# Earlier loads of transposed rows in linear attention, and attention weights copied to PSUM for VectorE's weighing

## The chip, the cores and the metric

The kernel runs on one core of one Trainium2 chip. A core has TensorE (PE, matrix multiplications, with its weight loads shown apart as PEld), VectorE (DVE), ScalarE (ACT), GpSimd (POOL) and SyncE (SP), each with its own instruction stream, and 16 DMA engines that move data between HBM and the on-chip memories SBUF and PSUM. Streams are in order: an instruction that waits holds up what stands behind it on its engine. The metric is the device time of one execution in microseconds (us).

## The reference

One block of a graph network over 6250 nodes with 256 features and 200000 edges sorted by destination. Cut to what matters:

```python
xn = layernorm(x)
x = x + gnn(xn, edge_index) + mix(xn)
x = x + ffn(layernorm(x))            # 8 experts, top 2

# gnn: three layers; heads 4, 4, 1
xh = (h @ W).reshape(n, heads, d)
alpha = leaky_relu((xh * att_src).sum(-1)[src] + (xh * att_dst).sum(-1)[dst])
e = exp(alpha - segment_max(alpha, dst)[dst])
alpha = e / segment_sum(e, dst)[dst]
out = segment_sum(xh[src] * alpha[:, :, None], dst)   # then + bias, layernorm, residual, relu

# mix: linear attention, 8 heads of 32
q, k, v = split(xn @ Wqkv.T);  q, k = elu(q) + 1, elu(k) + 1
kv = einsum("shd,shm->hmd", k, v)
t = q . kv / (q . sum(k))
x1 = layernorm(t + xn) ;  y = gelu(x1 @ W1.T + b1) @ W2.T + b2
mix = layernorm(y + x1)
```

## The kernel before

**Stages.** After planning the edges and projecting the nodes for the first layer (up to about 190 us), the kernel runs the three graph layers one after the other. The edges are laid out in rows of 128; 32 rows make a supertile, and each layer has 52 supertiles, worked in 16 steps each by `sum_messages`. A step takes two rows of edges.

**One supertile.** POOL gathers the rows of source nodes by indirect DMA, one instruction for each row of 128 edges (`gather`, L536), into tiles `g` of eight rows; 8 such tiles are in turn in layer 0, 9 in layer 1. The next gather into a tile waits until PE has read it. From the gathered scores the generator `maxima` computes the softmax weights of the supertile ahead, in pieces that are advanced in steps 9 to 14: ACT copies the scores out of `g` (L593), PE and VectorE take running maxima (L603 to L655), VectorE forms the exponents `w` (L666), ACT takes the exponential (L678), and VectorE writes each row's turn values into `g` (L684). In layers 0 and 1 (4 heads) `weigh` then multiplies the gathered rows with `w`: of each four rows ACT does two (L700, one instruction for each head), VectorE the other two in one instruction (L693). PE sums the rows by destination with one-hot matrices (`pair`, L730), which VectorE makes by comparing lane numbers (L559); for that comparison a copy of the lane numbers, `lane_ps`, lies in PSUM. VectorE adds the sums to `acc` (L743). Layer 2 has one head, and there ACT weighs all rows.

**Work beside.** Everything else is cut into pieces by `yield`, and `Beside.step` takes pieces from a queue at each step, in layer 0 at 1.25 pieces a step. In layer 0 the queue first holds `linear_attention`, then the updates of blocks of nodes as they are complete; in layer 2 it holds the experts. `Order` keeps on each engine the order of the text.

**Linear attention.** Two passes over 13 groups of node blocks (the first of one block, the others of four). Each group's normalized, transposed rows come from HBM (`xnt`) into the tile `et` by `load_xt`. The first pass forms keys and values (L1050) and sums their product; the second forms queries (L1106) into `qt`, multiplies (L1115), normalizes, transposes the result into `at` (another use of the tile `et`, L1138), runs the two layers W1 (L1145, into `ht`, another use of the tile `qt`) and W2 (L1154, with `at` added by L1157), normalizes again and stores the group to `res`. All these tiles have one buffer. In both passes the load stands at the head of a group; the loads are issued on SP, in the order of the text, so in the second pass it comes behind the store of the group before (L1169):

```python
    for g, (t0, n) in enumerate(groups()):      # second pass, L1090
        w = n * P
        xt = load_xt(g, n)
        x = wk.tile([P, GRP, C + 2 * HEADS], F32, name="ea")[:, :, :C]
        Where(tc, t0, n).load(x, i["x"])
        yield
```

Of the kernel before, what the change touches and what calls it, by code (L numbers as in the profile page):

```python
# [7 lines left out]
F32 = mybir.dt.float32  # L8
# [5 lines left out]
PS = bass.MemoryType.PSUM  # L14

P = 128
# [22 lines left out]
GRP = 4  # L39
# [433 lines left out]
def sum_messages(tc, pools, consts, q, node_rows, adn, h, acc, beside, slot, order):  # L473
# [7 lines left out]
    nc = tc.nc  # L481
    lp, tb, gp, hp, tp, wk, pmp, smp = pools
# [7 lines left out]
    half = GRP // 2 if h > 1 else 0  # L490
# [14 lines left out]
    T, A, M = {}, {}, {}  # L505
# [90 lines left out]
    def maxima(s):  # L596

        m, t = M[s], T[s]
# [3 lines left out]
        at = smp.tile([P, P], F32, name="sm")  # L602
# [62 lines left out]
        w = m["w"] = wk.tile([P, h, SU], F32, name="w")  # L665
# [12 lines left out]
        nc.scalar.activation(w, w, AF.Exp)  # L678
        nc.scalar.activation(fac, fac, AF.Exp)
        yield  # L680

        for k in range(subs):
            i = slice(k * SUB, (k + 1) * SUB)
# [4 lines left out]
    def weigh(s, c, n, engine):  # L688

        t, k, w = rows[s * subs + c // SUB], c % SUB, M[s]["w"]  # L690
        if engine is nc.vector:
            x = t[:, k:k + n, :body].rearrange("p c (h d) -> p c h d", h=h)
            nc.vector.tensor_tensor(  # L693
                x, x, w[:, :, c:c + n].rearrange("p h c -> p c h")[:, :, :, None].to_broadcast(
                    [P, n, h, d1]), op=OP.mult)
            return
        for i in range(n):
            for j in range(h):
                x = t[:, k + i, j * d1:(j + 1) * d1]
                nc.scalar.activation(x, x, AF.Copy, scale=w[:, j, c + i:c + i + 1])  # L700
# [57 lines left out]
    for s in range(-1, NS):  # L758
        n = s + 1
# [202 lines left out]
def groups():  # L962

    return [(0, 1)] + [(t0, GRP) for t0 in range(1, NB, GRP)]
# [60 lines left out]
def linear_attention(tc, pools, consts, i, mean, rstd, xnt, res):  # L1025

    nc = tc.nc
    mp, wk, sm, psum = pools
# [9 lines left out]
    def load_xt(j, n):  # L1038
        xt = wk.tile([P, 2, GRP * P], F32, name="et")
        load(tc, xt[:, :, :n * P], xnt[j, :, :, :n * P])  # L1040
        return xt

    for g, (t0, n) in enumerate(groups()):
        xt = load_xt(g, n)
        yield
        pk = psum.tile([P, 2, P + 1], F32, name="fk")
        for t in range(n):
            pt = psum.tile([P, 512], F32, name="fa")
            for k in range(2):
                nc.tensor.matmul(pt, xt[:, k, t * P:(t + 1) * P], wkv[:, k, :],  # L1050
                                 start=(k == 0), stop=(k == 1))
            yield
            low = elu_low(tc, wk, pt[:, :C])
            val = wk.tile([P, 2, P + 1], F32, name="val1")
            nc.vector.memset(val[:, :, P:], 1.0)
            nc.scalar.copy(val[:, :, :P], pt[:, C:].rearrange("p (j d) -> p j d", j=2))
            yield
            key = wk.tile([P, C], F32, name="key1")
            elu_join(tc, pt[:, :C], low, key)
            if t0 + t == 0:  # L1060
                nc.vector.memset(key[:SHIFT], 0.0)
            yield
            for j in range(2):
                nc.tensor.matmul(pk[:, j, :], key[:, j * P:(j + 1) * P], val[:, j, :],
                                 start=(t == 0 and j == 0), stop=(t == n - 1 and j == 1))
        yield
        nc.vector.tensor_add(kvs, kvs, pk)
# [4 lines left out]
    for j in range(2):  # L1072
        for q in range(4):
            s = slice(q * 32, (q + 1) * 32)
# [14 lines left out]

    for g, (t0, n) in enumerate(groups()):  # L1090
        w = n * P
        xt = load_xt(g, n)
        x = wk.tile([P, GRP, C + 2 * HEADS], F32, name="ea")[:, :, :C]
        Where(tc, t0, n).load(x, i["x"])
        yield
        qt = wk.tile([P, 2, GRP * P], F32, name="qt")
        pts, low = {}, None
        for j in range(3):
            if low is not None:
                elu_join(tc, pts[j - 2][:, :w], low, qt[:, j - 2, :w])  # L1100
            if j:
                low = elu_low(tc, wk, pts[j - 1][:, :w])
            if j < 2:
                pts[j] = psum.tile([P, 512], F32, name=("fa", "fk")[j])
                for k in range(2):
                    nc.tensor.matmul(pts[j][:, :w], wq[:, k, j * P:(j + 1) * P], xt[:, k, :w],  # L1106
                                     start=(k == 0), stop=(k == 1))
            yield
        elu_join(tc, pts[1][:, :w], low, qt[:, 1, :w])
        yield  # L1110
        a = wk.tile([P, GRP, C], F32, name="eo")
        for t in range(n):
            pt = psum.tile([P, 2, P + 4], F32, name=("fa", "fk")[t % 2])
            for j in range(2):
                nc.tensor.matmul(pt[:, j, :], qt[:, j, t * P:(t + 1) * P], kvm[:, j, :],  # L1115
                                 start=True, stop=True)
            yield
            z = sm.tile([P, 2, 4], F32, name="z")
            nc.vector.tensor_scalar(z, pt[:, :, P:], 1e-6, None, op0=OP.add)
            nc.vector.reciprocal(z, z)  # L1120
            nc.vector.tensor_tensor(
                a[:, t, :].rearrange("p (j h d) -> p j h d", j=2, d=32),
                pt[:, :, :P].rearrange("p j (h d) -> p j h d", d=32),
                z[:, :, :, None].to_broadcast([P, 2, 4, 32]), op=OP.mult)
            xn = wk.tile([P, C], F32, name="xn")
            nc.vector.tensor_scalar(xn, x[:, t, :], mean[:, t0 + t, 0:1],
                                    rstd[:, t0 + t:t0 + t + 1], op0=OP.subtract, op1=OP.mult)
            nc.vector.tensor_add(a[:, t, :], a[:, t, :], xn)
        yield
        yield from norm_pieces(tc, sm, consts, a, n)  # L1130
        at = wk.tile([P, 2, GRP * P], F32, name="et")
        for k in range(2):
            pt = psum.tile([P, 512], F32, name=("fa", "fk")[k])
            for t in range(n):
                nc.tensor.transpose(pt[:, t * P:(t + 1) * P], a[:, t, k * P:(k + 1) * P],
                                    consts["ident"])
            yield
            nc.scalar.activation(at[:, k, :w], pt[:, :w], AF.Identity,  # L1138
                                 scale=cols["ln1_g"][:, k:k + 1], bias=cols["ln1_b"][:, k:k + 1])
        yield  # L1140
        ht = wk.tile([P, 2, GRP * P], F32, name="qt")
        for j in range(2):
            pt = psum.tile([P, 512], F32, name=("fa", "fk")[j])
            for k in range(2):
                nc.tensor.matmul(pt[:, :w], w1[:, k, j * P:(j + 1) * P], at[:, k, :w],  # L1145
                                 start=(k == 0), stop=(k == 1))
            yield
            nc.scalar.activation(ht[:, j, :w], pt[:, :w], AF.Gelu, bias=cols["b1"][:, j:j + 1])
        yield
        for t in range(n):  # L1150
            s = slice(t * P, (t + 1) * P)
            pt = psum.tile([P, 512], F32, name=("fa", "fk")[t % 2])
            for k in range(2):
                nc.tensor.matmul(pt[:, :C], ht[:, k, s], w2[:, k, :], start=(k == 0), stop=False)  # L1154
            nc.tensor.matmul(pt[:, :C], ones[0:1, :], b2, start=False, stop=False)
            for k in range(2):
                nc.tensor.matmul(pt[:, k * P:(k + 1) * P], at[:, k, s], consts["ident"],  # L1157
                                 start=False, stop=(k == 1))
            yield
            nc.scalar.copy(a[:, t, :], pt[:, :C])  # L1160
        yield
        yield from norm_pieces(tc, sm, consts, a, n)
        row(tc, a[:, :n], ln2_g, n, OP.mult)
        yield
        row(tc, a[:, :n], ln2_b, n, OP.add)
        yield
        nc.vector.tensor_add(a[:, :n], a[:, :n], x[:, :n])
        yield
        Where(tc, t0, n).store(res, a)  # L1169
# [3 lines left out]
def graph_block(ctx, tc, i, out):  # L1173
    nc = tc.nc
# [3 lines left out]
    consts = make_consts(tc, cp)  # L1178
# [28 lines left out]
    with tc.tile_pool(name="ord", bufs=1) as tmp, \  # L1207
# [6 lines left out]
        n = unordered(tc, tmp, psum, consts, i["dst"])  # L1214
# [19 lines left out]
    for l, h in enumerate(heads):  # L1234
        W = C + 2 * h
        with ExitStack() as lc:
            def pool(name, bufs, **kw):
                return lc.enter_context(tc.tile_pool(name=name, bufs=bufs, **kw))
# [3 lines left out]
            nc.vector.memset(acc, 0.0)  # L1242
            lp, tb, gp = pool("lay", 1), pool("tables", 4), pool("rows", (8, 9, 7)[l])
            hp, tp, wk = pool("hots", 4), pool("hots_t", 3), pool("scores", 2)
            consts["lane_ps"] = pool("lane_ps", 1, space=PS).tile([P, P], F32, name="lane_ps")
            nc.vector.tensor_copy(consts["lane_ps"], consts["lane"])
            pmp, smp = pool("pm", 3, space=PS), pool("smp", 2, space=PS)
            ew, es, eps_ = pool("nodes", 1), pool("nodes_sm", 2), pool("nodes_ps", 1, space=PS)
            mw = pool("moe_w", 3) if l == 2 else None
# [358 lines left out]
```

## Time and profile before

| | |
|---|---|
| median of 3 runs | 7555.33 us (7549.93 to 7557.84) |
| the profiled execution | 7542.13 us, span 7540.3 us |
| busy, share of the span | PE 76%, PEld 52%, DVE 62%, ACT 46%, POOL 66% |
| granted TensorE clock, mean | 0.823 |
| gathers in layers 0, 1, 2 | from 188 to 2470, 2544 to 4737, 4807 to 7358 us |
| HBM read, written | 1024.89 MB, 56.03 MB |

The span is the time from the first to the last instruction of one profiled execution; busy time is the sum of an engine's instruction rows. Rows of the profile's groups give line, engine, operation, tiles (out<-in, buffer numbers left out), shapes and count, then busy us and the mean ns of one, then the engine's idle time just before them and what ended most of it. In timelines each row has start us, duration us, and in brackets the idle time before it and what ended it. "issue" is time in which the engine waited for nothing that the profile shows. Answers for a single line give the shortest, median and longest duration in ns.

### The profile page before, as it was taken

To read this page: it belongs to the slowest core of one execution; us is meant where nothing else is said; L and a number is where in the kernel's file an instruction comes from. 1 tells how busy PE (TensorE), PEld (TensorE's weight loads), DVE (VectorE), ACT (ScalarE), POOL (GpSimd) and SP (SyncE) were. 2 spreads that over 40 slices of the span, in tenths; PEclk is the share of its full clock that TensorE was granted. 3 is DMA by queue.
4 is the path that set the end of the run, shared out by engine and by line. 5 is a ranking of instruction groups with operands and counts; after the bars stand their busy time and mean duration, and the time that the engine had idled before them with its cause. 6 is when DMAs were issued, how large, how long until landed. Compare 5 with 4: busy or idle time off the path is not lost. (4 is left out here: it accounts for less than half of the span.)

```text
span 7540.3 us, 99268 instructions
## 1 busy us (share of the span) xinstructions
PE 5705.6 (76%) x24919; PEld 3900.4 (52%) x24919; DVE 4692.9 (62%) x13293; ACT 3442.0 (46%) x10810; POOL 4995.5 (66%) x5019
## 2 busy tenths in 40 slices
PE   5687878777766366666666666369999999999998
PEld 3455545455444244434444444246666666666666
DVE  5567777788866466656666666455555655555552
ACT  2455555555444244444444444234545544544543
POOL 0777666677777477777777777476665666666660
PEclk8798888877777677777777777679999999999999
DMA  4555444455555454545545555455555555555563
GB/s 149 151 156 151 134 141 132 141 146 162 150 147 133 90 145 138 143 137 146 143 140 146 141 146 135 90 142 163 165 158 157 160 154 155 158 154 161 159 149 90
DMA packets 627785, 1086.34 MB, mean 144 GB/s; under 512 B 200127, under 2 KB 355155, under 8 KB 627198
## 3 DMA queue, kind: packets, MB, share of 16 engines
q0 software_dynamic: 240288, 671.72, 33.9%
q1 hardware_dynamic: 386910, 408.03, 18.1%
q8 instruction: 217, 3.56, 0.2%
q14 instruction: 370, 3.03, 0.1%
HBM read 1024.89 MB, written 56.03 MB: 143 GB/s over the span
## 5 line engine op out<-in xcount | busy, mean ns | idle before, releaser
L536 POOL DMA_INDIRECT g<-node_rows,src_t x4992 | 4979.1, 997 | 2298.4 <-issue 1362.2
L730 PE MATMUL pm<-g,hot 128*128 128x264 f32 (+1 forms) x9984 | 3281.1, 463 | 759.6 <-ACT g L700 396.8
L730 PEld LDWEIGHTS pm<-g,hot 128*128 128x128 f32 x9984 | 2080.4, 224 | 1484.0 <-ACT g L700 491.6
L700 ACT ACTIVATE g<-g,w 128x65 f32<-128x65 f32 (+1 forms) x8320 | 2399.3, 369 | 0.1
L743 DVE TENSOR_TENSOR acc<-acc,pm 128x264 f32 (+1 forms) x2496 | 1048.6, 420 | 222.1 <-PE pm L730 199.9
L593 ACT COPY asc<-g 128x32 f32<-128x32 f32 (+1 forms) x624 | 140.5, 225 | 1609.8 <-DMA g<-node_rows,src_t 1609.6
L559 DVE TENSOR_TENSOR hot<-lane_ps,lane_t 128x1024 f32<-128x1024 f32 x624 | 758.6, 1216 | 0.0
L607 DVE TENSOR_TENSOR_SCAN mx_f<-cut_t,sm 128x128 f32<-128x128 bf16 (+1 forms) x156 | 64.6, 414 | 953.9 <-PE sm L603 953.7
L693 DVE TENSOR_TENSOR g<-g,w 128x520 f32<-128x520 f32 x832 | 575.4, 692 | 3.7 <-issue 1.4
L603 PE MATMUL sm<-ident,asc 128*128 128x128 f32 (+1 forms) x156 | 59.8, 383 | 586.3 <-ACT asc L593 586.2
L586 PEld LDWEIGHTS <-hot_t 128*128 128x128 bf16 x4992 | 310.3, 99 | 281.6 <-DVE hot_t L551 75.4
L1524 ACT ACTIVATE moe_h<-fa,moe_b 128x512 f32<-128x512 f32 (+1 forms) x208 | 137.7, 662 | 614.8 <-PE fa L1519 614.2
L1531 PE MATMUL fa<-moe_w,moe_h 128*128 128x256 f32 x1600 | 394.5, 389 | 17.3 <-ACT moe_h L1524 15.5
L1519 PE MATMUL fa<-et,moe_w 128*128 128x512 f32 (+1 forms) x832 | 394.8, 598 | 6.5 <-DVE eo L1536 4.0
L1519 PE MATMUL fk<-et,moe_w 128*128 128x512 f32 (+1 forms) x832 | 382.3, 582 | 15.4 <-DVE eo L1536 8.0
L1531 PE MATMUL fk<-moe_w,moe_h 128*128 128x256 f32 x1536 | 372.1, 385 | 0.9 <-DVE eo L1536 0.9
L586 PE MATMUL sm<-adc,hot_t 128*128 128x12 bf16 (+1 forms) x4992 | 325.1, 178 | 45.8 <-DVE hot_t L551 40.5
L603 PEld LDWEIGHTS sm<-ident,asc 128*128 128x128 f32 (+1 forms) x156 | 23.0, 147 | 649.4 <-ACT asc L593 647.4
L1531 PEld LDWEIGHTS fa<-moe_w,moe_h 128*128 128x128 f32 x1600 | 293.4, 191 | 66.3 <-ACT moe_h L1524 24.5
L551 DVE TENSOR_SCALAR hot_t<-hot_t,pidx 128x1024 bf16<-128x1024 bf16 x624 | 301.6, 483 | 37.4 <-DMA hot_t<-q_lane_rows 37.1
L1531 PEld LDWEIGHTS fk<-moe_w,moe_h 128*128 128x128 f32 x1536 | 283.0, 190 | 39.4 <-DVE eo L1536 1.7
L1536 DVE SCALAR_TENSOR_TENSOR eo<-fa,share,eo 128x256 f32<-128x256 f32 x200 | 96.1, 481 | 317.8 <-PE fa L1531 317.5
(370 smaller groups left out, 5643.5 us busy)
## 6 DMA issues: line engine op xcount, KB each, us to landing
hot_t<-q_lane_rows SPq DMA_DIRECT2D x624, 256.0 KB
moe_w<-in_L_ffn_W_dram SPq DMA_DIRECT2D x208, 512.0 KB
g<-node_rows,src_t POOLq DMA_INDIRECT x4992
ea<-node_rows SPq DMA_DIRECT2D x24, 528.0 KB
et<-xnt SPq DMA_DIRECT2D x24, 512.0 KB
hid<-eo SPq DMA_DIRECT2D x24, 512.0 KB
eold<-hid SPq DMA_DIRECT2D x24, 512.0 KB
node_rows<-r SPq DMA_DIRECT2D x12, 528.0 KB
```

The costliest lines, as they stand in the source:

```text
L536: nc.gpsimd.indirect_dma_start(out=t[:, c, :], out_offset=None, in_=node_rows, in_offset=bass.IndirectOffsetOnAxis(ap=T[s]["src"][:, i:i + ...
L551: nc.vector.tensor_scalar(lanes[m], lanes[m], consts["pidx"], None, op0=OP.is_equal)
L559: nc.vector.tensor_tensor(t, consts["lane_ps"][:, None, :].to_broadcast([P, SUB, P]), T[s]["lane"][:, k * SUB:(k + 1) * SUB, None].to_broa ...
L586: nc.tensor.matmul(m["ex"][:, c], lanes[s * subs + c // SUB][:, c % SUB, :], adc(s)[:, :, :, c // 2], start=True, stop=True)
L593: nc.scalar.copy(m["asc"][:, :, k * SUB:(k + 1) * SUB].rearrange("p h c -> p c h"), rows[s * subs + k][:, :, body:])
L693: nc.vector.tensor_tensor(x, x, w[:, :, c:c + n].rearrange("p h c -> p c h")[:, :, :, None].to_broadcast([P, n, h, d1]), op=OP.mult)
L700: nc.scalar.activation(x, x, AF.Copy, scale=w[:, j, c + i:c + i + 1])
L730: nc.tensor.matmul(pm, m["hots"][2 * i // SUB][:, k + j, :], t[:, k + j, :], start=(j == 0), stop=(j == 1))
L743: nc.vector.tensor_tensor(at, at, pm, op=OP.add)
L1519: nc.tensor.matmul(pt[:, :w], w1[:, k, j * P:(j + 1) * P], xt[:, k, :w], start=(k == 0), stop=(k == 1))
L1524: nc.scalar.activation(hx[:, j, :w], pt[:, :w], AF.Gelu, bias=self.b1[:, e * 4 + j:e * 4 + j + 1])
L1531: nc.tensor.matmul(pt[:, :C], hx[:, j, t * P:(t + 1) * P], w2[:, j, :], start=(j == 0), stop=(j == 3))
```

## The change

In `linear_attention` the load of a group's transposed rows moves from the head of the group to the end of the group before it, behind the last matmul that reads the tile. The first load, and the one for the second pass's first group, have places of their own; in the first pass one `yield` stands before the loop in place of one in each group. In the second pass `at` and `ht` swap tiles, so that the tile `et` is free for the next rows after the last L1154 of a group. In `maxima`, for layers with more than one head, VectorE copies `w` after the exponential into PSUM, into one of two halves by turns, and VectorE's weighing reads that copy; ACT's weighing reads `w` as before. The PSUM tile of the lane numbers grows by these two halves, within its bank.

```diff
 # maxima
         nc.scalar.activation(w, w, AF.Exp)
         nc.scalar.activation(fac, fac, AF.Exp)
         yield
+        if half:
+            m["w_ps"] = consts["w_ps"][:, s % 2].rearrange("p (h c) -> p h c", h=h)
+            nc.vector.tensor_copy(m["w_ps"], w)
 
 # weigh
         if engine is nc.vector:
+            w = M[s].get("w_ps", w)
             x = t[:, k:k + n, :body].rearrange("p c (h d) -> p c h d", h=h)
 
 # linear_attention, first pass
+    xt = load_xt(0, 1)
+    yield
     for g, (t0, n) in enumerate(groups()):
-        xt = load_xt(g, n)
-        yield
...
                 nc.tensor.matmul(pt, xt[:, k, t * P:(t + 1) * P], wkv[:, k, :],
                                  start=(k == 0), stop=(k == 1))
+            if t == n - 1:
+                xt = load_xt(g + 1, GRP) if g + 1 < len(groups()) else load_xt(0, 1)
             yield
 
 # linear_attention, second pass
         w = n * P
-        xt = load_xt(g, n)
...
-        at = wk.tile([P, 2, GRP * P], F32, name="et")
+        at = wk.tile([P, 2, GRP * P], F32, name="qt")
...
-        ht = wk.tile([P, 2, GRP * P], F32, name="qt")
+        ht = wk.tile([P, 2, GRP * P], F32, name="et")
...
                 nc.tensor.matmul(pt[:, k * P:(k + 1) * P], at[:, k, s], consts["ident"],
                                  start=False, stop=(k == 1))
+            if t == n - 1 and g + 1 < len(groups()):
+                xt = load_xt(g + 1, GRP)
             yield
 
 # graph_block
-            consts["lane_ps"] = pool("lane_ps", 1, space=PS).tile([P, P], F32, name="lane_ps")
+            ps = pool("lane_ps", 1, space=PS).tile([P, 3, P], F32, name="lane_ps")
+            consts["lane_ps"] = ps[:, 0]
             nc.vector.tensor_copy(consts["lane_ps"], consts["lane"])
+            consts["w_ps"] = ps[:, 1:]
```

## The prediction

> **What bounds the kernel now.** I read the page's busy table and costliest groups first, then the busy time by stage, then what the gathers waited for in each stage, then single gathers beside VectorE. The page:
>
> ```profile
> PE 5705.6 (76%) x24919; PEld 3900.4 (52%) x24919; DVE 4692.9 (62%) x13293; ACT 3442.0 (46%) x10810; POOL 4995.5 (66%) x5019
> ...
> L536 POOL DMA_INDIRECT g<-node_rows,src_t x4992 | 4979.1, 997 | 2298.4 <-issue 1362.2
> L693 DVE TENSOR_TENSOR g<-g,w 128x520 f32<-128x520 f32 x832 | 575.4, 692 | 3.7 <-issue 1.4
> ```
>
> No engine is busy throughout, and POOL's 66% hides that it is the bound for half of the span: of its idle time 1362.2 us are "issue", a pause behind each gather in which it waits for nothing. Busy time by stage (columns: window, its us, then PE, PEld, DVE, ACT, POOL; the windows are layer 0 with attention's first pass, attention's second pass, layer 0's rest, layer 1, layer 2):
>
> ```profile
> 260.00:700.00 440.00, 359.87 (x1633) 235.19 (x1631) 295.53 (x866) 245.32 (x918) 335.06 (x345) 0.90 0.55 151
> 700.00:1500.00 800.00, 620.56 (x2731) 411.70 (x2731) 586.41 (x1596) 424.10 (x1394) 540.44 (x547) 0.82 0.49 139
> 1500.00:2480.00 980.00, 682.89 (x2910) 470.24 (x2910) 720.78 (x1992) 470.02 (x1747) 737.98 (x717) 0.73 0.55 146
> 2600.00:4700.00 2100.00, 1351.88 (x5867) 901.10 (x5866) 1353.90 (x3683) 911.79 (x3632) 1613.89 (x1596) 0.74 0.51 142
> 4900.00:7350.00 2450.00, 2277.47 (x10008) 1592.39 (x10009) 1403.25 (x4195) 1183.44 (x2524) 1553.70 (x1584) 0.94 0.56 157
> ```
>
> In layer 1 one gather starts every 2100/1596 = 1.316 us. The gather's own row for 2700 to 4600 us shows what of that is unavoidable:
>
> ```profile
> L536 POOL DMA_INDIRECT g<-node_rows,src_t x1444: 942/946/2479, 2699.3 to 4599.2; - x181
> ...
>   issue: 384.2, 1261
> ```
>
> Median 946 ns, and 0.30 us of pause behind each: 1.25 us at best. The pauses never exceed that pair in layer 1 (summed excess over 304 ns: 1.1 us), while ACT's L593 waits 791 us for gathers to land. So layer 1 is bound by POOL, and so are the first window (excess pause 0.2 us) and the third (14 us). The second isn't: there POOL's pauses exceed 304 ns by 94 us, waiting for row buffers that PE has not yet read. Layer 2 is bound by PE.
>
> Why do gathers take 1012 ns on average in layer 1 where the median is 946? POOL and then VectorE at one place (start, duration):
>
> ```profile
> 3150.05 1.49 POOL L536 DMA_INDIRECT g<-node_rows,src_t  x1 [0.30 <-issue]
> 3151.85 0.94 POOL L536 DMA_INDIRECT g<-node_rows,src_t  x1 [0.30 <-issue]
> ```
>
> ```profile
> 3150.03 0.69 DVE L693 TENSOR_TENSOR g<-g,w 128x520 f32<-128x520 f32 x1
> 3150.64 0.42 DVE L743 TENSOR_TENSOR acc<-acc,pm 128x264 f32 x1
> 3150.98 1.21 DVE L559 TENSOR_TENSOR hot<-lane_ps,lane_t 128x1024 f32<-128x1024 f32 x1
> ```
>
> The gather at 3150.05 is 0.54 us too long: L693 was running 0.13 us after its start and ended at 3150.72, 0.54 us after that point. The next gather starts inside L559, which is twice as long but reads one operand from PSUM, and takes 0.94 us. Going through all gathers with that rule (which VectorE row is under way 128 ns after the start) the excess over 946 ns is what is left of that row: the match is within 60 ns for 309 of 397 gathers under L693. Excess under L693: 91.9 us in all, of which 6.3, 9.9, 25.4 and 48.3 us fall in the first four windows. Under L743 (reads PSUM): 4 ns each over 573 gathers; under L559: nothing that counts.
>
> The second pass of attention, at one of its twelve boundaries between groups:
>
> ```profile
> 1032.06 0.41 SPq L903 DMA_DIRECT2D res<-eo  x1
> 1032.58 0.43 SPq L903 DMA_DIRECT2D et<-xnt  x1
> ```
>
> ```profile
> 1030.61 2.10 PE L730 MATMUL pm<-g,hot 128*128 128x264 f32 x4 [0.52 <-ACT g L700]
> 1037.06 3.78 PE L1106 MATMUL fa<-et,wq 128*128 128x512 f32 x4 [4.35 <-DMA et<-xnt]
> ```
>
> The load of transposed rows stands in SP's queue behind the store of the finished group; PE comes to L1106 and stands 4.35 us, and VectorE after it idles 5.96 us until its first L1022.
>
> **The change, part by part.**
>
> *Second-pass loads.* The load moves up to the group's last L1154/L1157 matmuls, on SP past the store and ahead of the x load. It now waits for PE to finish reading ht, which lives in the same tile. At this boundary those matmuls start at 1011.2 and end at 1013.4; landing takes the 4.5 us seen above, so rows are there at 1018, 15 us before 1032.7, when PE wants them. If that cover went, the 4.3 us would come back. Behind the load on SP are hot_t loads, which wait for later PE steps anyway. Removed: PE's waits at the eleven boundaries from 728 to 1488 us, 45.7 us in sum (window 700 to 1500, row of L1106). The one before, 5.3 us at 659, lies where POOL is the bound, and counts nothing. POOL's floor for the window is 547 x (1.25 + 0.04) = 706 us of 800, so it can follow. Between 0 (the next wait, ACT's table loads or the scan chain, takes over) and 94 us (all of POOL's pauses): I take the 45.7 us of the waits themselves.
>
> *First-pass loads.* Same move; eight waits of L1050, 30.6 us, go, but POOL has no free moment there: 0. Next in line is the load itself: it has four pieces, 3.2 steps of 2.55 us = 8 us, against 4.5 us. Twelve yields fewer bring the second pass forward by 9.6 steps, about 24 us; the number of steps is fixed, and layer 0's updates have caught up by about 2090 us (after that they follow at the pace at which blocks complete), so this alone yields nothing.
>
> *at and ht swap tiles.* No instruction more; each tile's last reader lies a stage back, as before: 0.
>
> *L693 with w in PSUM.* Gathers no longer stretch under it. Where POOL is the bound that is a gain in full: 6.3 + 25.4 + 48.3 + about 1.5 at the layer ends = 81.5 us. In the second pass POOL isn't the bound: 0 of 9.9. A rule speaks against this part: the Trainium skill (SBUF — State Buffer, Who interferes with whom) says that an operation with two SBUF inputs contends with GpSimd's reads of SBUF, but infers from a probe that tensor_tensor does not stall descriptor generation, which needs the write interface. By that, L693 stretches nothing and moving w frees nothing: 7555 - 38 = 7517 us. The rows here show the stretch under L693 and none under L559, so I take the rows.
>
> *L693's own length.* The skill (VectorE: DVE Perf Modes, The TRN2 errata) gives a PSUM source 62 cycles more fixed cost than an SBUF source: an estimate from that page of 65 ns, or 8.7 us for the 134 L693 of the second pass, where VectorE may matter (7444 us instead of 7435). The trace: L559 with one PSUM operand 1216 ns for 1024 elements, L1386 with none 1215. I take 0.
>
> *The copy of w.* 52 in each of layers 0 and 1, SBUF to PSUM, 128x128: lane_ps<-lane at L1246 is the same operation, 275 to 289 ns. 104 x 0.29 = 30 us of VectorE, beside POOL in three windows (VectorE is idle 36% of layer 1), so 0 there; some 17 in the second pass, 5 us, charged in full. It waits for ACT's Exp of w, and behind it in VectorE's order stand L684, L693 and the next L743, on which PE waits. In layer 1 Exp ended at least 1.2 us before VectorE came to L684, in all 52 cases; in layer 0 it came late in about one case in ten, 12.6 us in sum, one of them 6 us. Between 0 and 12.6 I charge 3 us, since L693 a step later waited for the same Exp. In layer 2 no copy is made.
>
> Sum: 45.7 - 8 + 81.5 = 119 us, taken as 120. Against the profiled execution, 7542.1 us (span 7540.3), that is 7422; the median of the runs shown is 13 us above it, so 7555 - 120 = 7435 us.
>
> **The rivals.**
> 1. Only the weighing pays, since another wait takes the place of L1106's: 7555 - 75 = 7480. For it: PE still idles beside the maxima chain (2.1 us before L655 at 1023), and much of it stays. Against it: L1106 starts a chain that VectorE and ACT (10.7 us idle) both wait for.
> 2. Only attention pays, POOL being stretched by something else in the same stretch: 7555 - 38 = 7517. Against it: L559 and L743.
> 3. Slower: VectorE stands at the copy for ACT's Exp, and everything behind it. Place: end of step 14 of each supertile. To eat 120 us and 15 us more it would have to stand 1.3 us at each of 104 copies; the trace gives 12.6 us in sum. It decides only if ACT, which waited 4.2 us for w at 1026, becomes the late one. About 7575.
> 4. Both gains vanish behind a common bound: no change. A difference of 0.2%, 15 us, is about what can be told from none.
>
> **How the numbers follow.** Both parts pay: 0.72, its own range 7395 to 7470 (second pass 20 to 75 us, weighing 60 to 90). Rival 1: 0.13. Rival 2: 0.07. No change: 0.03. Slower: 0.05. The range 7380 to 7490 holds the first two. Faster 0.92, same 0.03, slower 0.05.
>
> **What would show it.** Right: in layer 1 the mean gather falls from 1012 to about 980 ns with the median still 946, pitch 1.285 us, no gather stretched under the weighing; L1106 without a DMA wait, and the second pass 40 to 50 us shorter; the copy at 0.29 us. Wrong: gathers as long as before under the weighing; the weighing at over 0.75 us; VectorE waiting for ACT ahead of the copies by tens of us; POOL's pauses in layer 1 over 304 ns.

## The result, and the profile after

| | before | after |
|---|---|---|
| median of 4 runs | 7555.47 us | 7424.51 us |
| ratio, 95% interval | | 0.9828 (0.9815 to 0.9842) |
| span of the profiled execution | 7540.3 us | 7423.7 us |
| mean granted TensorE clock | 0.823 | 0.831 |

The kernel became 131 us faster by the medians and 117 us by the two profiled executions. The page of the kernel after, the rows that answer to those of before:

```profile
PE 5681.9 (77%) x24919; PEld 3887.8 (52%) x24919; DVE 4734.3 (64%) x13397; ACT 3445.8 (46%) x10811; POOL 4912.9 (66%) x5019
...
L536 POOL DMA_INDIRECT g<-node_rows,src_t x4992 | 4896.4, 981 | 2263.0 <-issue 1356.7
...
L697 DVE TENSOR_TENSOR g<-g,lane_ps 128x520 f32<-128x520 f32 x832 | 571.5, 687 | 8.0 <-issue 6.0
```

The mean gather went from 997 to 981 ns over all layers. The weighing, now L697, takes 687 ns where it took 692, so its operand in PSUM does not lengthen it. VectorE's 104 instructions more are the copies. One place on POOL and then VectorE:

```profile
3098.26 0.95 POOL L536 DMA_INDIRECT g<-node_rows,src_t  x1 [0.30 <-issue]
```

```profile
3097.72 0.68 DVE L697 TENSOR_TENSOR g<-g,lane_ps 128x520 f32<-128x520 f32 x1
3098.33 0.42 DVE L747 TENSOR_TENSOR acc<-acc,pm 128x264 f32 x1
```

This gather begins while the weighing is under way (until 3098.40) and takes 0.95 us. There are 403 gathers whose start plus 128 ns falls inside a weighing; their mean is 949 ns, and their time over 946 ns is 1.4 us in all. Counted in the same way, 441 gathers of the kernel before carried 94 us.

A boundary between two groups of attention's second pass, on SP and then PE:

```profile
965.66 0.34 SPq L907 DMA_DIRECT2D et<-xnt  x1
969.85 10.42 SPq L907 DMA_DIRECT2D hot_t<-q_lane_rows  x3
980.36 0.39 SPq L907 DMA_DIRECT2D res<-eo  x1
```

```profile
979.76 2.11 PE L734 MATMUL pm<-g,hot 128*128 128x264 f32 x4
981.66 0.31 PE L586 MATMUL sm<-adc,hot_t 128*128 128x12 bf16 x4
981.82 3.12 PE L1111 MATMUL fa<-et,wq 128*128 128x512 f32 x4
```

The rows are fetched 15 us ahead of the store that used to hold the load, and L1111 (L1106 before) follows L586 without a pause.

To see where the time went I cut both traces at the same gathers, counted from the first of a layer (1664 in each). Times are from one gather's start to another's; "stretch" is the sum over 946 ns, "pauses" that over 304 ns between two gathers:

| stage | before | after | stretch, before and after | pauses, before and after |
|---|---|---|---|---|
| layer 0, gathers 0 to 416 | 532.0 us | 525.5 us | 11.7, 5.2 | 0.3, 0.3 |
| layer 0, 416 to 1040 (second pass) | 915.2 | 859.8 | 32.6, 21.4 | 102.6, 58.5 |
| layer 0, 1040 to the last | 833.9 | 814.0 | 50.1, 28.6 | 4.5, 6.1 |
| layer 1 | 2191.8 | 2148.4 | 106.0, 61.5 | 6.6, 7.9 |
| layer 2 | 2550.1 | 2551.6 | 56.2, 57.3 | 415.1, 415.4 |

The gains are 6.5, 55.4, 19.9 and 43.4 us, 125 us; layer 2, what lies between the layers and both ends give back 9. In layers 0 and 1 outside the second pass POOL has almost no pauses to lose, and the gain there is about the stretch that went. In the second pass it is mostly pauses. The second pass by engine, before and after (window, its us, then busy us of PE, PEld, DVE, ACT and POOL with their instructions, the granted TensorE clock, DMA share, GB/s):

```profile
719.70:1634.80 915.10, 705.89 (x3070) 470.74 (x3068) 681.71 (x1870) 478.86 (x1584) 622.86 (x624) 0.80 0.49 138
```

```profile
714.00:1573.80 859.80, 699.62 (x3098) 472.14 (x3097) 696.27 (x1912) 486.12 (x1604) 611.62 (x624) 0.83 0.53 146
```

Slightly more work in 55 us less: what went is mainly idle time of PE (from 209 to 160 us), VectorE (233 to 164) and ACT (436 to 374) together. The granted clock is also higher, 0.83 where it was 0.80; the first experiment comes back to that.

### The profile page after: what moved, and what is told of

Read it like the earlier page. It is cut to its first block, busy times and chain, and to the rows that moved or that the text cites. A ratio compares the mean times of both kernels' runs of the same rounds, so it can differ in the third digit from the quotient of the medians.

```text
span 7423.7 us, 99384 instructions
## 1 busy us (share of the span) xinstructions
PE 5681.9 (77%) x24919; PEld 3887.8 (52%) x24919; DVE 4734.3 (64%) x13397; ACT 3445.8 (46%) x10811; POOL 4912.9 (66%) x5019
## 5 line engine op out<-in xcount | busy, mean ns | idle before, releaser
L536 POOL DMA_INDIRECT g<-node_rows,src_t x4992 | 4896.4, 981 | 2263.0 <-issue 1356.7
L559 DVE TENSOR_TENSOR hot<-lane_ps,lane_t 128x1024 f32<-128x1024 f32 x624 | 760.4, 1219 | 0.0
L697 DVE TENSOR_TENSOR g<-g,lane_ps 128x520 f32<-128x520 f32 x832 | 571.5, 687 | 8.0 <-issue 6.0
L586 PEld LDWEIGHTS <-hot_t 128*128 128x128 bf16 x4992 | 314.6, 100 | 297.4 <-DVE hot_t L551 82.5
L586 PE MATMUL sm<-adc,hot_t 128*128 128x12 bf16 (+1 forms) x4992 | 326.8, 178 | 51.8 <-DVE hot_t L551 47.5
L551 DVE TENSOR_SCALAR hot_t<-hot_t,pidx 128x1024 bf16<-128x1024 bf16 x624 | 308.7, 495 | 42.4 <-DMA hot_t<-q_lane_rows 42.1
```

What stands on the lines that cost most here:

```text
L536: nc.gpsimd.indirect_dma_start(out=t[:, c, :], out_offset=None, in_=node_rows, in_offset=bass.IndirectOffsetOnAxis(ap=T[s]["src"][:, i:i + ...
L551: nc.vector.tensor_scalar(lanes[m], lanes[m], consts["pidx"], None, op0=OP.is_equal)
L559: nc.vector.tensor_tensor(t, consts["lane_ps"][:, None, :].to_broadcast([P, SUB, P]), T[s]["lane"][:, k * SUB:(k + 1) * SUB, None].to_broa ...
L586: nc.tensor.matmul(m["ex"][:, c], lanes[s * subs + c // SUB][:, c % SUB, :], adc(s)[:, :, :, c // 2], start=True, stop=True)
L697: nc.vector.tensor_tensor(x, x, w[:, :, c:c + n].rearrange("p h c -> p c h")[:, :, :, None].to_broadcast([P, n, h, d1]), op=OP.mult)
```

## The experiments

All ratios are to the kernel before, run on the same chip beside each experiment.

### One part at a time

The loads alone: the diff without its hunks in `maxima` and `weigh`; the larger PSUM tile of graph_block stays, with its new halves unused.

> Only the earlier loads and the tile swap; VectorE weighs from SBUF as before. Theory (the two parts act on different stages and add): layer 0's second pass gives 40 to 55 us, nothing else moves: 7500 to 7515 us, layer 1 as long as before (gathers over 2193 us), its mean gather about 1010 ns. Rival A (the second pass became shorter because the gathers no longer stretch there): under 15 us, 7540 or more. Rival B (removing L1106's waits is what makes POOL the bound everywhere): over 75 us.

Measured: 7478.94 us, ratio 0.9912 (0.9890 to 0.9934), 68 us less than before. The second pass takes 849.7 us, 65.5 less than before; layer 1 is as before (2193.8). The place was right and the size too small. The rows of L1106 in that stage, of the kernel before and of this one (there L1107):

```profile
L1106 PE MATMUL fa<-et,wq 128*128 128x512 f32 x44 | 41.0, 1087 | 45.7 <-DMA et<-xnt 45.7
L1106 PE MATMUL fk<-et,wq 128*128 128x512 f32 x44 | 22.7, 641 | 0.0
```

```profile
L1107 PE MATMUL fa<-et,wq 128*128 128x512 f32 x40 | 27.2, 817 | 0.0
L1107 PE MATMUL fk<-et,wq 128*128 128x512 f32 x40 | 19.6, 612 | 0.0
```

The stage gained more than PE's waits. Its 65.5 us are, on PE, 59.3 us less idle time (209.2 to 149.9 us), of which the waits for rows are 45.7, and 6.2 us less busy time, with 22 matmuls more. VectorE's idle time fell by 71 us (233 to 163).

PE was busy for less because its matmuls ran faster on average: the fa matmuls took 1087 ns before and take 817 now, about 12 us for 44 of them. Most take either about 592 or about 1061 ns, the first of four somewhat more. The wait alone is not what makes them slow. These rows of the kernel before show the granted clock ahead of one wait and behind it (0.50 and 1.00), and matmuls behind it:

```profile
1022.00:1032.00 10.00, 7.00 (x16) 4.63 (x17) 9.62 (x25) 3.39 (x14) 6.11 (x6) 0.50 0.34 95
1042.00:1052.00 10.00, 10.00 (x75) 7.50 (x73) 6.70 (x18) 7.47 (x30) 4.13 (x5) 1.00 0.40 109
```

```profile
1044.14 1.05 PE L730 MATMUL pm<-g,hot 128*128 128x264 f32 x4
```

Four L730 matmuls took 2.10 us at 1030.61, ahead of the wait that ended at 1037.06 (the row is in the prediction), and 1.05 us at 1044.14. At nine of the eleven boundaries the clock was at 0.50 before PE began to wait. With no wait left, PE still enters six of ten boundaries at the slow speed in this kernel, and eight of ten in the full change. How much of the gain beyond the 45.7 us comes with the higher granted clock (0.803 to 0.825 in this stage), and how much from other waits that became shorter, was not separated.

The copy of w alone: the hunks in `maxima`, `weigh` and graph_block, loads as before.

> Only the copy of w in PSUM and VectorE's weighing from it; loads as before. Theory (lock between an operation with two SBUF inputs and the gather's descriptor work): layer 1 shorter by 43 us as in the full change, layer 0 outside the second pass by 25 us, second pass by 0 to 12: 7475 to 7490 us, no gather stretched under the weighing. Rival A (additive with a larger share in the second pass, since stretches there reach PE later): 7465 to 7475. Rival B (the gain in layer 1 came from elsewhere): 7540 or more.

Measured: 7491.23 us, ratio 0.9925 (0.9898 to 0.9952), 55 us less. Layer 1 takes 2150.1 us (41.7 less), with hardly any stretch under the weighing (1 us); layer 0's first and last parts give 2.5 and 16.4 us; the second pass takes 927.5 us, 12 more than before, though its gathers' stretch fell from 32.6 to 21.3. POOL's pauses there rose from 102.6 to 126.2 us instead. The two ratios multiplied give 0.984, the full change 0.983: within the intervals the parts add.

### The place of the operand

The full change with the copy in SBUF:

```diff
-            consts["w_ps"] = ps[:, 1:]
+            consts["w_ps"] = lp.tile([P, 2, P], F32, name="w_copy")
```

> The full change with the copy of w in a second SBUF tile in place of PSUM: same instructions, same waits, same order. Theory (the place of the operand is what counts): the weighing stretches gathers again by 80 to 90 us in sum and the time goes back to 7490 to 7510 us. Rival (the copy helps by freeing w's buffer or by shifting VectorE's order): stays within 10 us of the full change, 7415 to 7435.

Measured: 7486.46 us, ratio 0.9918 (0.9894 to 0.9942): the gain of the loads alone and nothing else. Layer 1 takes 2195.2 us. The rows of its 2700 to 4500 us:

```profile
L536 POOL DMA_INDIRECT g<-node_rows,src_t x1365 | 1385.6, 1015 | 415.8 <-issue 366.5 <-DVE ends L612 12.2 <-PE pm L734 9.4
...
L697 DVE TENSOR_TENSOR g<-g,w_copy 128x520 f32<-128x520 f32 x342 | 237.1, 693 | 1.3 <-issue 0.4
```

The order of instructions is that of the full change; the memory differs, and with it the length of one copy (0.23 us where it is 0.29). The mean gather is back at 1015 ns (1013 in the kernel before, in the same window). So the gain of the copy comes from its place.

### Another operation with two SBUF inputs

The full change with the lane numbers of L559 read from SBUF:

```diff
-            t, consts["lane_ps"][:, None, :].to_broadcast([P, SUB, P]),
+            t, consts["lane"][:, None, :].to_broadcast([P, SUB, P]),
```

> The full change with the lane numbers of L559 read from SBUF: now this 1.22 us operation, 416 times in layers 0 and 1 each 208, has two SBUF inputs. Dose test. Theory (a gather that starts its read inside such an operation waits for its end): by the square of the length, 1.22 against 0.69 us, each costs 3.1 times a weighing; there are 624 in all, 208 in each layer against 416 weighings. Weighing cost 44 us in layer 1, so L559 should cost about 44 x 3.1 / 2 = 68 us in layer 1, about 65 in layer 0, little in layer 2, which PE bounds: 7540 to 7580 us. Rival (something in the weighing itself, its writes into the gathered tiles, stretches the gathers): no stretch under L559, 7415 to 7440.

Measured: 7558.03 us, ratio 1.0021 (1.0014 to 1.0028), 134 us above the full change by the medians, and slightly slower than the kernel before. Layer 1 takes 2217.3 us, 69 more than in the full change, where 68 was expected from the lengths alone. POOL and VectorE at one place:

```profile
2753.15 2.00 POOL L536 DMA_INDIRECT g<-node_rows,src_t  x1 [0.30 <-issue]
```

```profile
2753.11 1.23 DVE L559 TENSOR_TENSOR hot<-lane,lane_t 128x1024 f32<-128x1024 f32 x1
```

L559 ends at 2754.34, 1.06 us after the gather's start plus 0.13, and the gather is 1.06 us over its 0.946. The two agree within 60 ns for 478 of 496 gathers under L559. L559 writes other tiles than the weighing does, so it is not the gathered tile that matters. In the second pass the stretch under L559 is 41.7 us and the stage takes 860.8 us against 859.8: POOL's pauses fell from 58.5 to 20.0 and took it all. So POOL is not the bound there.

### First-pass loads

The full change with the loads of the first pass at the head of each group again:

```diff
-    xt = load_xt(0, 1)
-    yield
     for g, (t0, n) in enumerate(groups()):
+        xt = load_xt(g, n)
+        yield
...
-            if t == n - 1:
-                xt = load_xt(g + 1, GRP) if g + 1 < len(groups()) else load_xt(0, 1)
+            if t == n - 1 and g + 1 == len(groups()):
+                xt = load_xt(0, 1)
```

> The full change, but in attention's first pass each group's load stands at its head again, with its yield. Theory (POOL bounds the first pass, so its waits cost nothing): within 5 us of the full change, the first 416 gathers in 525 us as there, though PE waits about 25 us for these loads again. Rival (the waits there or the twelve pieces more do count, since the loads alone shortened layer 0's last third by 9 us): 10 us or more above the full change, 7435 or more.

Measured: 7415.85 us, ratio 0.9829 (0.9812 to 0.9845), as the full change. PE waits 27.3 us for these loads again, and the first 416 gathers take 524.5 us. These waits of PE cost nothing, as POOL is the bound there.

### The copy, once more

The full change with each copy made twice:

```diff
             nc.vector.tensor_copy(m["w_ps"], w)
+            nc.vector.tensor_copy(m["w_ps"], w)
```

> The full change with the copy of w made twice in a row, 104 instructions of 0.29 us more on VectorE. Theory (the second pass is bound by the chain of waits among PE, VectorE and ACT, and a copy in that chain delays it; elsewhere POOL hides it): the second pass (gathers 416 to 1040) 5 to 12 us longer than the 860 us of the full change, layer 1 within 3 us of 2148. Rival (what the copy costs is its wait for ACT's Exp, which a second copy doesn't wait for): no stage moves by more than 3 us.

Measured: 7423.78 us, ratio 0.9843 (0.9828 to 0.9858). The second pass takes 859.7 us, layer 1 2150.7: no stage moved by more than 3 us, as the rival said. The time of the instruction is free even in the second pass.

The full change without copies in layer 0's supertiles 13 to 31, where the second pass runs:

```diff
-        if half:
+        if half and not (gp.bufs == 8 and 13 <= s < 32):
```

> The full change without copies in supertiles 13 to 31 of layer 0, where attention's second pass runs; VectorE weighs from SBUF there. Theory (in that pass stretched gathers cost nothing and the copy does): the second pass in 848 to 853 us, as with the loads alone, in place of 860; all else as in the full change: 7412 to 7420 us. Rival (the stretch and the copy cost the same there, or the difference was chance): within 4 us of the full change.

Measured: 7408.54 us, ratio 0.9823 (0.9809 to 0.9836). The second pass takes 854.4 us, 5.4 less than in the full change and less of a gain than expected; the intervals of the two kernels overlap. The rival of the doubled copy, the wait for ACT's Exp, is not enough to explain the difference. These are the copies, and how long VectorE stood for Exp before them and how often, in the full change and in the kernel with the copy in SBUF:

```profile
L683 DVE COPY lane_ps<-w x104: 280/289/296, 240.0 to 4639.9; 128x128 f32<-128x128 f32 x104
...
  ACT w L678: 5.7, 4
```

```profile
L683 DVE COPY w_copy<-w x104: 215/225/441, 236.7 to 4696.0; 128x128 f32<-128x128 f32 x104
...
  ACT w L678: 6.7, 5
```

The waits are alike, yet with the copy in SBUF the second pass takes 852.8 us. Over all kernels with the early loads, it takes 857.5 to 860.8 us where the weighing in it reads PSUM (five kernels) and 849.7 to 854.4 us where it reads SBUF (four). These are single profiled executions, and a few us of one stage are not beyond chance; why the second pass is longer with the operand in PSUM stays open.

### The load just ahead of the store

The kernel before with its load moved across one line of the text:

```diff
+    xt = load_xt(0, 1)
     for g, (t0, n) in enumerate(groups()):
         w = n * P
-        xt = load_xt(g, n)
...
+        if g + 1 < len(groups()):
+            xt = load_xt(g + 1, GRP)
         Where(tc, t0, n).store(res, a)
```

> The kernel before, with one line moved: in attention's second pass the load of the next group's transposed rows is issued just ahead of the store of the finished group, in the same piece, in place of just behind it; tiles, first pass and weighing as before. Theory (SP is far ahead of the other engines and stands at the store, which waits for VectorE's last sum; the load waits for nothing that is late): L1106 waits no more, the second pass falls from 915 to 850 to 860 us, 7480 to 7495 us. Rival (what counts is how many pieces lie between load and matmul): the load comes only the store's 0.5 us earlier, the second pass gains 5 to 10 us: 7535 or more.

Measured: 7523.76 us, ratio 0.9962 (0.9949 to 0.9976). The second pass takes 879.6 us: 35.6 less, between the two expectations, so neither was right. SP at one boundary:

```profile
867.20 0.50 SPq L903 DMA_DIRECT2D joins_t<-q_joins  x1
867.82 0.34 SPq L903 DMA_DIRECT2D et<-xnt  x1
876.03 0.40 SPq L903 DMA_DIRECT2D res<-eo  x1
```

Here SP was early, and the load left 8.2 us ahead of the store that used to hold it. At other boundaries SP was still busy with hot_t loads, and came to load and store at once; in this stage six waits of L1106, 19.5 us, are left of eleven with 45.7. So 26.2 us of waits taken away gave 35.6 us, and all 45.7 gave 65.5 us in the kernel with the loads alone: by these two executions each microsecond of this wait was worth about 1.4.

### A faster version

The same stretch lies under the update's large products (22 us of it in layers 0 and 1 of the full change). In `Layer.update` the last small product can write into the free quarter of the lane numbers' bank, which needs no further instruction:

```diff
+        consts["ws_at"] = 1 - consts.get("ws_at", 1)
+        wp = consts["ws_ps"][:, consts["ws_at"] * 64:][:, :2 * GRP * h].rearrange(
+            "p (k n h) -> p k n h", k=2, n=GRP)
         for k in range(2):
-            nc.vector.tensor_mul(ws[:, k, :n], ws[:, k, :n], rz[:, :n])
+            nc.vector.tensor_mul(wp[:, k, :n], ws[:, k, :n], rz[:, :n])
+        ws = wp
...
+            consts["ws_ps"] = ps[:, 3]
```

> The full change, and the last product of the update's two weights (32 numbers a partition at most) is written to PSUM, so that the two large products with them (ea<-ea,own_w and eo<-acc,own_w, 1024 elements each) have one SBUF input. No instruction more. Theory (lock): no gather stretched under these two; 21 us of stretch go in layers 0 and 1, layer 1 shorter by 10 to 14 us, layer 0 by 5 to 8, layer 2 unchanged: 7400 to 7410 us. Rival (the other large operations of the update stand back to back with these and take the stretch over): within 5 us of the full change.

Measured: 7391.81 us, ratio 0.9801 (0.9786 to 0.9815): 33 us under the full change by the medians. The kernel before was itself 9 us faster beside this run than beside the full change; by the ratios the gain is 20 us, which is about what was expected, and the two intervals just meet. Layer 1 takes 2135.8 us (12.6 less than the full change), layer 0's last part 803.4 (10.6 less); no stretch is left under the two products, and layer 2 is not shorter (2556.5).

> The best version so far, put together: the full change, the update's weights in PSUM (as in e8), no copies in layer 0's supertiles 13 to 31 (as in e9). Theory (both act at different places and add; 33 and 16 us below the full change's median in their runs): 7375 to 7390 us. Rival (e9's gain was chance): as e8, 7390 to 7400.

Measured: 7401.26 us, ratio 0.9799 (0.9785 to 0.9812): the same ratio as with the update's weights in PSUM alone, close to what the rival had. The stages of layers 0 and 1 add up to 4318.0 us against 4322.2; leaving the copies out in the second pass is worth too little to be told.

## Why the prediction was right

The forecast was 7435 us for the likeliest case; measured were 7424.5. Profile to profile the sum was 119 us and the change gave 117. Its two main mechanisms hold, but two terms were off in opposite directions (the second pass gave 18 us more, the stages outside it 12 less), and 9 us were given back elsewhere, so that a total within 2 us is in part luck:

- **What bounds which stage**: right. Layer 1 and layer 0's ends follow the gathers; stretch added there is paid in full (L559: 69 us in layer 1), while the second pass absorbs it (41.7 us of stretch, 1 us of time).
- **Second-pass loads, 45.7 us**: too small; alone they gave 65.5, and with the copy 55.4, where 40 to 50 was named as the sign of being right. The term counted PE's waits for rows only. PE's other idle time fell by another 14 us and its busy time by 6, the latter with a higher granted clock; what caused these 20 us was not separated. The bound from above, 94 us of pauses, held.
- **First-pass loads, 0**: right; with the loads at the head again nothing moved. (Of the eight waits counted, 30.6 us, one of 2.6 us is that of a weight load; PE's matmuls wait seven times, 27.9 us.)
- **The weighing's stretch, 81.5 us**: too large; the stages outside the second pass gave 69.8 us, and 9 of the gain in layer 0's last part come with the loads alone too (824.6 us, with 10 us less stretch). The stretch under the weighing went as expected, from about 50 us to at most 1 in layer 1, but the total fell by 44.5 there: under other operations it grew by 5 us, which the sum took as fixed. Alone, the copy gave 61 us outside the second pass. The mean gather in layer 1 came to 983 ns, about the 980 that was forecast.
- **The copy, 8 us in the second pass**: the size was near (10 us against the loads alone), the split was wrong: it had 5 us for the instruction, and a second copy costs nothing. The other 3 us were for its wait, which was 5.7 us; but the copy in SBUF waited 6.7 us and cost 3. Where the rest comes from stays open.
- **The weighing's own length, 0**: right, 687 ns against 692.
- **The rule weighed against the rows**: the Trainium skill (SBUF — State Buffer, Who interferes with whom) infers why tensor_tensor did not stall descriptor generation in a probe. Here two of its uses lengthen indirect gathers, and the measurement decides: with a copy in SBUF a gather takes 1012 ns on average over layer 1, in PSUM 983. What the same section says of two SBUF inputs, that they contend with GpSimd's reads of SBUF, agrees.
- **Rivals**: none came about. The slower one needed 1.3 us of waiting at each of 104 copies; the sum was 5.7 us.

## What to carry to other kernels

Where GpSimd issues gathers back to back, look at the spread of their durations, not at the mean: a median of 946 ns beside rows of 1.3 to 2 us says that something else holds them, and here the VectorE row under way at their start named it. An operand that many VectorE operations read again can be worth a place in PSUM where the gathers are the bound, if a bank has room for it that only VectorE uses, as here (the Trainium skill, PSUM — Partial Sum Buffer, PSUM bank collisions raise a hardware error, warns of two engines in one bank; no run here tried that). A load that stands in a queue behind a store waited here for that store's data, and taking such waits away gained about 1.4 times their length in the second pass, where PE, VectorE and ACT wait for each other. First ask, by stage, which engine is the bound: the same kind of wait in the first pass cost nothing.

## What was not expected of the hardware

A gather is longer by what is left of a two-SBUF-input operation that is under way 128 ns after its start: within 60 ns for 309 of the 397 gathers under the weighing in the kernel before, and for 478 of 496 under L559 read from SBUF. Of the 1705 gathers of the kernel before with no VectorE row under way at that moment, none was over 60 ns too long. So the cost of such operations grows faster than their length: in layer 1, 208 of 1.22 us cost 69 us and 416 of 0.69 us 43 us, a factor of 3.2 for each one, where the square of their lengths gives 3.1. Over the whole kernel, 624 of 1.22 us cost as much as the whole change gave. L551, which reads one tile and a column of numbers, was also under way at some long gathers (13 us in the kernel before); that was not followed up.

PE's fa matmuls took 1061 ns or 592 ns, and slow ones stood at boundaries with no wait too: the granted clock had mostly been at 0.50 already when PE came to the wait.
